# Next tiles' norms on ScalarE, sums stored through SP's queue, lower parts on VectorE, in the first pair of a one-core attention and FFN kernel

## The chip, the cores and the metric

The kernel runs on one core of a Trainium2 chip. The time is the device time in microseconds (us) of that core, and the median of several runs is given. A run with the hardware profiler stands beside them; its page counts the span from the first to the last instruction.

The engines are called PE (TensorE), ACT (ScalarE), DVE (VectorE), POOL (GpSimd) and SP (SyncE, which here only issues DMAs). Each works through its own instructions in order. An instruction that waits holds up all that stand behind it on its engine, and that includes the DMAs which the engine issues.

## What is computed

The input has 4096 tokens of 256 values. Linear attention comes first, then a feed-forward network, each followed by a residual and a layer norm:

```python
Q, K, V = x @ wq.T, x @ wk.T, x @ wv.T          # 64 wide
energy  = K.T @ V                               # over all tokens
x = layernorm(x + (Q @ energy) * sqrt(3 / 64) @ wo.T)
h = silu((x @ w1.T) * s1) * ((x @ w2.T) * s2)   # 1024 wide
h = gelu((h @ h1.T) * hs1)                      # 1024 x 1024
h = gelu((h @ h2.T) * hs2)                      # 1024 x 1024
x = layernorm(x + (h @ w3.T) * s3)
```

## The kernel before

**Tiles and pairs.** The tokens are cut into eight tiles of 512, and these into four pairs. The attention runs first for all tiles, up to `m2 = energy @ wo`; the queries are kept in `stk`, with an upper part in rows 0 to 63 and a lower part in rows 64 to 127. Each pair then goes through the gate (`w1`, `w2`, 32 products), two square layers and the last product with `w3`. While a pair is in its gate, the attention's output of the next pair's tiles is added to `x` (`attend_norm`'s `add`); while it is in its square layers, these tiles are normalised, transposed by DVE in blocks of 32 and moved into `xT` by many small DMAs (`moves`).

**Two parts.** Matmuls run in a reduced float32 form, so an operand is split in two: `hi`, a cast on ACT, and `lo`, the rest, on DVE (`convert`, L231 and L232). Each product runs once with either.

**Square layers.** A 1024 x 1024 layer for a pair (1024 columns) is a 2 x 2 block product with seven block products instead of eight (`square_layer`). `ORDER` gives the order of the weights: A11, A12, S2, S1, S3, A22, S4, where the S are sums of blocks. A product (L278) uses two blocks of weights of 0.5 MB, 16 pairs of a weight load and a matmul of 128 x 512 for each, and writes four PSUM banks. Products 1, 3, 5 and 6 share the banks `al` (6, 7, 4, 5), and ACT reads these out after each: copies at L347, L361 and L371, and after product 6 the GELU of L318. Products 2, 4 and 7 use `be` (0 to 3). The next layer's product 1 starts `al` anew.

**Weights.** `fetch` keeps five buffers `ws` filled. In pair 0 the blocks A11, A12 and A22 come from the inputs through POOL's queue (L267); all else comes from the scratch `sw` in DRAM through SP's queue (L269). The sums in `sw` are made in pair 0: `sums(layer, k)` has four DVE additions (L290) of raw blocks into two buffers `so` and two stores (L440, on POOL's queue). There are two buffers `so` in all, so that sum k+1 waits for the stores of sum k. Layer 0's sums are made in the attention and the gate of pair 0, layer 1's inside layer 0 (`second_sums`), with `raw_blocks` loading what k+2 needs.

**Background.** `fill(us)` takes jobs from a list and emits them at four places of a square layer, up to a budget that `FILL`, or `FIRST` in the first layer of pair 0, sets. A job is half a sum, half a norm or half a tile's transposes. All order is that of the program; nothing is rearranged.

**Norms.** `attend_norm` gives the steps: `stats` (L145, L147), `root` (L85 on DVE, then a power on POOL, L86) and `norm` (L167). In the jobs, `norm` runs on POOL, one pass of subtract and multiply per 128 tokens. The last pair's closing phase has another form (`norm_on_act`, L958 and L959): two passes on ACT, one with a negated mean as its bias and one with the root as its scale.

## Time and profile before

| | |
|---|---|
| median of 3 runs | 651.78 us (651.54 to 656.1) |
| profiled execution | 653.67 us, its span 651.9 us |
| PE busy | 631.8 us (97%) |
| DVE busy | 496.1 us (76%) |
| ACT busy | 381.4 us (59%) |
| POOL busy | 233.1 us (36%) |
| mean granted clock of PE | 0.987 |
| DMA moved | 113.44 MB, mean 174 GB/s |

Busy shares are means over the whole span; the stage that the change touches, the first square layer of pair 0, takes 51 us of it (72.7 to 123.4). In a line of a timeline the columns are: start, duration, engine, line, operation, the tiles written and read, shapes, count, and in brackets the idle time before it with what ended it. In a line of the waits: who waited for whom, the sum in us, how often, the longest. In a line of the groups: busy time and mean ns of one, then the idle time before the group. In the windows each engine has its busy time and count, and PEclk is the share of full clock that PE was granted.

### The profile page before, as it was taken

How to read it: one execution, taken by the hardware profiler on the slowest of the kernel's cores; microseconds unless marked ns; L12 is line 12 of the kernel's file. 1: busy time of each engine (PE TensorE's matmuls, PEld its weight loads, DVE VectorE, ACT ScalarE, POOL GpSimd, SP SyncE). 2: the span in 40 equal slices, each digit the busy share in tenths (PEclk: the TensorE clock that was granted, in tenths of full speed). 3: DMA queues.
4: the chain of work that ended last, by engine and by line, in shares of the span. 5: the costliest groups of instructions: out<-in, count | busy, mean ns of one | idle time of the engine just before them, and what ended most of it. 6: DMA issues, size and time to landing. Idle time of an engine off the chain costs nothing.

```text
span 651.9 us, 8976 instructions
## 1 busy us (share of the span) xinstructions
PE 631.8 (97%) x3163; PEld 533.6 (82%) x3163; DVE 496.1 (76%) x750; ACT 381.4 (59%) x522; POOL 233.1 (36%) x290
## 2 busy tenths in 40 slices
PE   8999999959999999999999999999999999999994
PEld 7878888848898888888898888888899888888894
DVE  3789986895475888698677988798767987588466
ACT  5546472645664455655684556766684556766564
POOL 1234117722814713632535722631645720000005
PEclk9999999979999999999999999999999999999998
DMA  8988749845853037764762125654860125644201
GB/s 335 330 300 246 244 144 364 268 155 182 250 152 103 33 137 247 268 218 167 225 191 71 60 97 171 216 183 154 248 190 4 65 98 173 215 150 141 98 1 67
DMA packets 58800, 113.44 MB, mean 174 GB/s; under 512 B 19488, under 2 KB 34528, under 8 KB 58368
## 3 DMA queue, kind: packets, MB, share of 16 engines
q1 hardware_dynamic: 40864, 73.56, 34.0%
q0 software_dynamic: 17520, 38.55, 18.6%
q10 hardware_dynamic: 368, 0.72, 0.3%
q8 instruction: 26, 0.43, 0.3%
q14 instruction: 22, 0.18, 0.1%
HBM read 97.08 MB, written 18.87 MB: 178 GB/s over the span
## 4 chain that ended last, share of the span: by engine, by line
PE 86%; DMA 5%; DVE 5%; POOL 1%; issue 1%; ACT 1%; SPq 0%; POOLq 0%; DVEq 0%; ACTq 0%
PE bank L278 53%; PE bank L611 18%; PE bank L755 9%; DMA sw<-so 3%; PE bank L507 2%; DVE f L290 2%; PE bank L528 1%; DMA ws<-in_h 1%; POOL x L167 1%; DVE so L290 1%; DMA f<-in_xt 1%; PE bank L518 1%; PE bank L137 1%; PE bank L138 1%; DVE lo L232 1%
## 5 line engine op out<-in xcount | busy, mean ns | idle before, releaser
L278 PE MATMUL bank<-hi,ws 128*128 128x512 f32 x896 | 350.3, 391 | 7.7 <-DMA ws<-in_h 7.7
L278 PE MATMUL bank<-lo,ws 128*128 128x512 f32 x896 | 349.9, 391 | 0.0
L232 DVE TENSOR_TENSOR lo<-f,hi 128x1024 fp32r<-128x1024 f32 x144 | 170.3, 1221 | 69.6 <-ACT hi L231 69.1
L278 PEld LDWEIGHTS bank<-hi,ws 128*128 128x128 f32 x896 | 169.0, 189 | 43.3 <-DVE f L290 8.1
L278 PEld LDWEIGHTS bank<-lo,ws 128*128 128x128 f32 x896 | 169.1, 189 | 35.2
L231 ACT CAST hi<-f 128x1024 fp32r<-128x1024 f32 x144 | 144.5, 1051 | 52.0 <-PE bank L278 26.9
L318 ACT ACTIVATE f<-f,hs 128x512 f32<-128x512 f32 x96 | 62.8, 715 | 71.7 <-DVE f L290 71.7
L611 PE MATMUL bank<-hi,w 128*128 128x512 f32 (+1 forms) x268 | 101.7, 383 | 1.0 <-DVE d L766 0.6
L611 PE MATMUL bank<-lo,w 128*128 128x512 f32 (+1 forms) x268 | 101.2, 381 | 0.1
L620 ACT ACTIVATE f<-bank,s 128x512 f32<-128x512 f32 x64 | 44.0, 690 | 65.6 <-PE bank L611 62.3
L290 DVE TENSOR_TENSOR f<-f,f 128x1024 f32<-128x1024 f32 x64 | 76.5, 1221 | 4.5 <-ACT f L318 3.8
L290 DVE TENSOR_TENSOR f<-f,bank 128x512 f32<-128x512 f32 x96 | 62.1, 681 | 21.8 <-ACT f L371 16.0
L767 POOL TENSOR_TENSOR x<-x,d 128x256 f32<-128x256 f32 x31 | 27.0, 897 | 114.0 <-DVE d L766 113.9
L621 DVE SCALAR_TENSOR_TENSOR f<-bank,s,f 128x512 f32<-128x512 f32 x64 | 47.7, 748 | 26.2 <-PE bank L611 23.6
L755 PE MATMUL bank<-w,lo 128*128 128x256 f32 x256 | 61.6, 283 | 0.0
L755 PE MATMUL bank<-w,hi 128*128 128x256 f32 x256 | 61.6, 283 | 0.0
L611 PEld LDWEIGHTS bank<-hi,w 128*128 128x128 f32 x268 | 50.4, 188 | 11.3 <-DVE d L766 1.0
L611 PEld LDWEIGHTS bank<-lo,w 128*128 128x128 f32 x268 | 50.4, 188 | 9.6 <-DVE lo L191 0.3
L216 POOL DMA_DIRECT2D xT<-x x96 | 52.2, 551 | 8.1 <-DMA stage<-in_h 3.0
L755 PEld LDWEIGHTS bank<-w,lo 128*128 128x128 f32 x256 | 49.1, 192 | 0.2
L755 PEld LDWEIGHTS bank<-w,hi 128*128 128x128 f32 x256 | 49.1, 192 | 0.2
L717 POOL DMA_DIRECT2D stage<-in_h x16 | 9.0, 561 | 107.8 <-DVE stage L743 104.0
(121 smaller groups left out, 553.1 us busy)
## 6 DMA issues: line engine op xcount, KB each, us to landing
ws<-sw SPq DMA_DIRECT2D x100, 512.0 KB, 3.3
sw<-so POOLq DMA_DIRECT2D x16, 512.0 KB, 5.4
stage<-in_h POOLq DMA_DIRECT2D x16, 512.0 KB, 5.0
ws<-in_h POOLq DMA_DIRECT2D x12, 512.0 KB, 7.4
sw<-in_h SPq DMA_DIRECT2D x12, 512.0 KB, 5.5
x<-in_x SPq DMA_DIRECT2D x16, 256.0 KB, 3.7
f<-in_xt SPq DMA_DIRECT2D x6, 512.0 KB, 7.8
f<-in_h SPq DMA_DIRECT2D x6, 512.0 KB, 10.3
```

Source lines behind the costliest of these rows:

```text
L216: moves.popleft()()
L231: nc.scalar.copy(hi[:, c, :], src[:, c, :])
L232: nc.vector.tensor_tensor(lo[:, c, :], src[:, c, :], hi[:, c, :].bitcast(F32), ALU.subtract)
L278: nc.tensor.matmul(ps[2 * h + o], w[:, k, o * P : (o + 1) * P], part[i][:, k, :], start=start and k == 0 and i == 0, stop=k == HK - 1 and ...
L290: engine.tensor_tensor(dst, u, v, op)
L318: nc.scalar.activation(dst, src, AF.Gelu, scale=sc[:, o : o + 1])
L507: nc.tensor.matmul(pk[:, s, :], x[:, k, s * P : (s + 1) * P], wkv[:, k, :], start=(k == 0), stop=(k == KE - 1),)
L611: nc.tensor.matmul(ps[:, c], w[:, k, o * P : (o + 1) * P], part[:, 2 * j + k, c], start=(k == 0 and i == 0), stop=(k == KE - 1 and i == 1),)
L620: nc.scalar.activation(g, pa, AF.Silu, scale=s1[:, o : o + 1])
L621: nc.vector.scalar_tensor_tensor(g, pb, s2[:, o : o + 1], g, ALU.mult, ALU.mult)
L755: nc.tensor.matmul(ps[:, :E], part[q][:, k, s * P : (s + 1) * P], w3[:, k0 + k, :], start=i % 2 == 0 and k == 0 and q == 0, stop=i % 2 == ...
L767: engine.tensor_tensor(y[:, s, :], y[:, s, :], d, ALU.add)
```

## The change

1. In the first pair the norms of tiles 2 and 3 leave POOL: `norm_on_act` does them on ACT in two passes, after both halves' statistics; DVE makes the negated mean (`minus_mean`).
2. `sums` stores through SP's queue. The two sums made in the attention stay on POOL's. `raw_blocks` for layer 1 goes through SP for k = 0 and 2 and through POOL for 1 and 3.
3. The lower parts of query tiles 3, 4 and 5 (`stack_lo`) move from POOL to DVE, and from ahead of the gate to inside its first products.
4. The jobs' order is k0, k1, norm 2, k2, transposes 2, k3, norm 3, transposes 3, where the transposes stood at the end; `FIRST` has other budgets.
5. The activation that loads the Silu table at a pair's end is issued after the tail's GELU and not ahead of it.

```diff
+        def norm_on_act(minus):
+            for s in range(NS):
+                nc.scalar.activation(
+                    y[:, s, :], x[:, s, :], AF.Identity, bias=minus[:, s : s + 1], scale=1.0
+                )
+                nc.scalar.activation(
+                    y[:, s, :], y[:, s, :], AF.Identity, scale=r[s // 2][:, s % 2 : s % 2 + 1]
+                )
+
+        def minus_mean():
+            m = p2.tile([P, NS], F32, tag="mm", name=f"mm{t}")
+            nc.vector.tensor_scalar(m, mv[:, :, 0], -1.0, None, ALU.mult)
+            return m
+
+        norm.on_act = norm_on_act, minus_mean
...
-    FIRST = {2: 2.8, 3: 5.4, 4: 2.8, 5: 5.4}
+    FIRST = {2: 2.8, 3: 5.8, 4: 4.4, 5: 5.8}
...
-    def sums(layer, k, raw):
+    def sums(layer, k, raw, queue=nc.sync):
...
-            nc.gpsimd.dma_start(
+            queue.dma_start(
                 out=sw[layer][2 * i : 2 * i + 2, :, :, k, :].rearrange("m h p o -> p m h o"),
...
     def stack_lo(t):
-        nc.gpsimd.tensor_tensor(
+        nc.vector.tensor_tensor(
             stk[t][D:P], qf[t][D:P], stk[t][D:P].bitcast(F32), ALU.subtract
         )
...
-                early = sums(0, t // 2 - 2, raws[t // 2 - 2])
+                early = sums(0, t // 2 - 2, raws[t // 2 - 2], nc.gpsimd)
...
-    for t in range(3, LATE):
-        stack_lo(t)
...
         if o == 1:
             turn(2, 4)
             split(2, 4)
+            for t in range(3, LATE):
+                stack_lo(t)
...
-            raw_blocks(1, 0, xTr, nc.gpsimd)
+            raw_blocks(1, 0, xTr)
...
-                raw_blocks(1, k + 2, later_raws[k % 2], nc.gpsimd)
+                raw_blocks(1, k + 2, later_raws[k % 2], (nc.sync, nc.gpsimd)[k % 2])
...
-    def attend_jobs(t):
+    def attend_jobs(t, on_act=False):
...
             root(g)
+            if on_act:
+                if g:
+                    norms, minus = norm.on_act
+                    norms(minus())
+                return
             for s in (2 * g, 2 * g + 1):
                 norm(s, nc.gpsimd)
...
-            (a0, a1), (a2, a3) = attend_jobs(ta + 2)
-            (b0, b1), (b2, b3) = attend_jobs(tb + 2)
+            (a0, a1), (a2, a3) = attend_jobs(ta + 2, p == 0)
+            (b0, b1), (b2, b3) = attend_jobs(tb + 2, p == 0)
...
-                background.extend((*k0, *k1, a0, a1, *k2, *k3, b0, b1, a2, a3, b2, b3))
+                background.extend((*k0, *k1, a0, a1, *k2, a2, a3, *k3, b0, b1, b2, b3))
...
-        if p + 1 < NP:
-            nc.scalar.activation(once, mhalf[:, :1], AF.Silu)
...
         tail()
+        if p + 1 < NP:
+            nc.scalar.activation(once, mhalf[:, :1], AF.Silu)
```

As the program is emitted, PE's order stays as it was. On ACT the eight passes of tile 2 stand between the casts of product 6's operand and those of product 7's, ahead of the copies L371; the eight of tile 3 stand after the casts of the next layer's first operand and ahead of the GELU that reads product 6's banks. On DVE the negated mean follows each tile's statistics, tile 2's transposes stand between the halves of sums 2 and 3, and tile 3's after its statistics.

## The prediction

> **What bounds the kernel now.** The page gives TensorE (PE) 97% of the span, and the chain that ended last is 86% PE. So only PE's holes can move the time, and I read the waits of PE first:

> ```profile
> PE bank L278 <- DMA ws<-in_h: 7.7, 1, 7.7
> ...
> PE bank L182 <- DVE x L167: 0.7, 1, 0.7
> ```

> There is one large hole, 7.7 us, in a matrix product of the square layers (L278) that waits for a weight block. The windows around it say when, and that it costs more than its length:

> ```profile
> core 0: us, PE busy (x) PEld busy (x) DVE busy (x) ACT busy (x) POOL busy (x), PEclk, DMA share, GB/s
> ...
> 134.00:138.00 4.00, 0.48 (x3) 0.06 (x1) 3.43 (x3) 2.33 (x3) 1.04 (x2) 0.88 0.93 287
> 138.00:142.00 4.00, 0.00 (x0) 0.00 (x0) 3.97 (x5) 3.99 (x7) 0.00 (x0) 0.50 0.30 77
> 142.00:144.00 2.00, 1.79 (x4) 1.49 (x5) 2.00 (x3) 0.00 (x0) 0.00 (x0) 0.50 0.03 8
> ```

> PEclk falls to 0.50 in the hole and stays there after it. In the chain, the 176 matmuls after the hole take 42.54 us, and at 101.55 us for 448 (the rate of the later pairs) they would take 39.9: the half clock costs 2.6 us more. The hole is worth **10.3 us**.

> The POOL timeline shows why the block came late:

> ```profile
> 125.85 3.83 POOL L167 TENSOR_SCALAR x<-x,mv,ra 128x256 f32<-128x256 f32 x2
> 129.65 0.71 POOL L86 TENSOR_TENSOR ra<-ra,mhalf 128x2 f32<-128x2 f32 x1
> 130.47 3.78 POOL L167 TENSOR_SCALAR x<-x,mv,ra 128x256 f32<-128x256 f32 x2
> 134.19 0.85 POOL L267 DMA_DIRECT2D ws<-in_h  x1
> ```

> The block's fetch (L267) is queued on POOL behind the norms of tile 3. It was issued at 134.2 and landed 7.9 us later; its buffer had been free since about 120.

> I count **half products** (16 matmuls, 3.63 us, one weight block each) from the first square layer of pair 0. Half 0 starts at 72.7, half 10 at 108.9, half 14 (the second layer) at 123.4. The hole stands before half 17. Half 10 begins product 6, half 14 the next layer's product 1. Both write the `al` banks, and both must first see ScalarE (ACT) read `al` out.

> **The change, part by part.**

> *POOL loses the norms of tiles 2 and 3 and the later sum stores.* The late block now stands behind seven small moves (L216, 0.55 each) and two powers (L86, 0.8 each), which wait for tile 3's statistics and are over by about 130; 8 us of landing gives 138. The hole before half 17 goes: **-10.3 us**.

> *Three lower parts (L550) move from POOL to DVE.* While POOL ran them (37.5 to 41.3), DVE's norm of tile 0 was slow and PE waited for it. In DVE's timeline:

> ```profile
> 34.80 0.74 DVE L167 TENSOR_SCALAR x<-x,mv,ra 128x256 f32<-128x256 f32 x2 [0.26 <-POOL ra L86]
> ...
> 37.44 2.75 DVE L167 TENSOR_SCALAR x<-x,mv,ra 128x256 f32<-128x256 f32 x2
> ```

> and in PE's timeline

> ```profile
> 40.25 0.55 PE L182 MATMUL bank<-ident,x 128*128 128x128 f32 x3 [0.74 <-DVE x L167]
> ```

> The same two norms took 0.74 and then 2.75. With POOL idle the second pair ends near 38.2, before the transposes at 39.24 need it. The 0.74 and the 0.18 after it go, and I leave 0.1 for the split that follows: **-0.8 us**. On DVE the three operations (0.69 each by L539, the same 64x512) stand before the first gate's product at 43.55, in an idle stretch of 1.2 us. The gates' three pairs of banks hide the rest. Without that cover it would be 0.9.

> *Stores through SP.* Two queues are concerned. SP's loads of `x` for tiles 2 and 3 now wait behind the sums of the gate phase: issued at about 62 instead of 40 and 52. Before, the transfers of those microseconds filled the DMA engines, the last of the two issued at 61.5 and 62.05 landing at 67.7. One 0.5 MB transfer replaces another there, so the first `x` lands at about 67.7, just as DVE wants it (67.8). PE needs the add done at 69.9, and it ended at 69.1: 0, at most 2. Later SP's weight loads (L269) wait behind stores: the second one of product 7 behind the third step's first store, at 112 for a use at 120. Hidden.

> Does a store land sooner from SP? [...] The rows show nothing: `sw<-so` from POOL 5.4 us median, `sw<-in_h` from SP 5.5, same size. [...]

> *Norms on ACT.* The price is in the closing phase, which has this very pair of passes:

> ```profile
> L959 ACT ACTIVATE x<-x,ro 128x256 f32<-128x256 f32 x7 | 3.6, 509 | 0.6 <-POOL ro L86 0.2
> L958 ACT ACTIVATE x<-x,minus 128x256 f32<-128x256 f32 x7 | 3.5, 499 | 5.8 <-DVE minus L967 5.8
> ```

> Eight passes are 4.0 us. Busy time isn't the matter, place is. In ACT's new order tile 2's passes stand before the casts of product 7's operand (L231, 2.0) and the copies out of `al` (L371). Tile 3's stand before the GELUs out of `al` (L318). Where these were, in ACT's timeline:

> ```profile
> 103.69 0.59 ACT L371 COPY f<-bank 128x512 f32<-128x512 f32 x1 [0.95 <-PE bank L278]
> ...
> 119.12 2.40 ACT L318 ACTIVATE f<-bank,hs 128x512 f32<-128x512 f32 x4
> ```

> and the work that makes the norms ready, in DVE's timeline:

> ```profile
> 102.80 0.69 DVE L290 TENSOR_TENSOR so<-stk 128x512 fp32r<-128x512 f32 x1 [0.60 <-DMA sw<-so]
> ...
> 106.08 0.24 DVE L85 TENSOR_SCALAR ra<-mv 128x2 f32<-128x2 f32 x1
> ```

> ACT was idle there, but the norms are not ready there: the statistics stand on DVE behind sums 0 and 1, which wait for their buffers to be stored.

> Hole A, before half 10. Statistics end at 106.3 (the DVE row, and a negated mean of 0.15). Passes 4.0: 110.3. Casts 2.0: 112.3. First copy 0.59: 112.9. PE wanted it at 108.9, so it waits 4.0.

> Hole B, before half 14. DVE goes on when the casts are there: that operand's lower part to 114.2 (L232, ending 1.9 after the first cast); second half of sum 2 to 115.5 (two L290, 1.3); four transposes, moved up, to 117.0 (L815, 8.7/24 each); first half of sum 3 to 118.4; four adds of C22 to 120.9. Before, from the start of these adds to the end of the lower part of the next operand was 6.6 (114.05 to 120.66): 125.0. Second half of sum 3 to 126.3; statistics of tile 3 as at 123.70 to 126.08, and 0.15, to 128.8. Passes 4.0: 132.8. First GELU 0.68: **133.5**, where half 14 began at 123.4. So the second layer starts 10.1 later. Hole A, and a half clock after it, lie inside this, since the chain goes through DVE and ACT.

> PE is empty from about 129 to 133.5. What does the clock do? [...] The trace fell to half 2.6 us after the last matmul's end (134.5 to 137.0, from the 0.88) and lost 2.6. I take the row, 2.5. [...]

> *Silu load after the tail, FIRST, turn of queues.* Each of three pairs loses two table loads (1.28 each) on ACT; no wait of PE at a pair's turn names ACT, so 0. FIRST and the job order are already in the order used above.

> **Sum.** -10.3 - 0.8 + 10.1 + 2.5 = +1.5; the second layer's third product needs its operand at about 149, which the slow halves hide. Half 14's bounds: 130.6 if the stores land at once, so that statistics end at 104.0 (DVE's own work) and both chains shorten; 138 if two of the waited stores take 8.4 us, the slowest landing of this row, and not 4.7 to 5.7. That is -1.4 to +6, and up to 2 more for the `x` loads. Between, I allow 0.3 for an earlier issue (POOL issued the first store at 95.9, DVE had it ready at 95.6): **+1.2**. The profiled execution, 653.67 us (span 651.9), would be 654.9; the runs' median, 651.78, becomes **653.0**.

> **Rivals.**
> 1. *ScalarE hides the norms* (7%). Then both holes are absent: 651.8 - 11.1 = 640.7. For it: ACT is busy 59%, and sat idle 5.0 us before 114.76. Against: DVE's own work lets no passes start before 104, and 4 + 2 + 0.6 after that is 110.6, past 108.9.
> 2. *The stores are the bound* (16%). Sums 0 and 1, and then 2 and 3, share buffers; each step waits for a landing. From 98 to 112 the DMA engines are full (share 1.06 in that window from 100), and raw blocks, weights and stores now come from two queues. If two landings slip to 8.4 us and the `x` loads cost 1.5, half 14 starts at 138.5 and the sum is +8.0: 659.8. It decides, and makes the kernel slower by over 1%, from half 14 at 138.5, or at 137 with that delay of `x`.
> 3. *Forecast* (77%): hole 17 traded for holes A and B, 649 to 658.

> **How the numbers follow.** One per cent, 6.5 us, is about what a measurement of this kernel can tell from no change. Faster 0.07 is rival 1; slower 0.16 is rival 2, with the later `x` loads; same 0.77. The range, 648.5 to 660.5, takes in the bounds of half 14 (650.4 to 657.8), the `x` loads and rival 2's 659.8.

> **What would show it.** Waits of PE: no `ws<-in_h`, instead ACT before products 6 and 1, about 4 and 4.5 us; PEclk 0.50 near 130 to 137; ACT rows of L318 out of `bank` after eight passes, near 133; the transpose at 40.25 without its wait. I am wrong if PE has no hole at half 14, if its hole comes from a DMA, or if PE waits for `x` at 68.

## The result, and the profile after

The changed kernel takes 660.98 us (659.01 to 663.14) beside 651.66 of the kernel before: a ratio of 1.0139, with a 95% interval of 1.0097 to 1.0182. It is **slower by 1.4%**. The forecast was 653.0 with a range that ended at 660.5. The profiled execution took 662.13 us, its span 660.35, 8.5 more than before.

The waits of PE, who waited for whom, us in total, times, longest:

```profile
PE bank L294 <- ACT f L334: 6.6, 1, 6.6
...
PE bank L294 <- ACT f L387: 3.3, 1, 3.3
```

The wait of 7.7 us for `ws<-in_h` is gone, and so is the one of 0.7 before the transpose. In their place stand holes A (for the copies out of `al`, L387, which was L371) and B (for the GELUs out of `al`, L334, which was L318). The windows around hole B:

```profile
core 0: us, PE busy (x) PEld busy (x) DVE busy (x) ACT busy (x) POOL busy (x), PEclk, DMA share, GB/s
...
132.00:136.00 4.00, 0.00 (x0) 0.00 (x0) 1.75 (x8) 2.79 (x7) 3.57 (x6) 0.90 1.06 276
136.00:140.00 4.00, 2.39 (x6) 1.91 (x7) 0.89 (x2) 3.97 (x8) 3.71 (x8) 0.50 0.63 140
```

PE stands empty to 137.6, and the clock is at half there. ACT's timeline shows the eight passes ahead of what PE waits for, twice:

```profile
107.98 0.51 ACT L175 ACTIVATE x<-x,mm 128x256 f32<-128x256 f32 x1 [8.83 <-DVE mm L184]
...
111.88 1.97 ACT L247 CAST hi<-f 128x1024 fp32r<-128x1024 f32 x2
113.76 2.04 ACT L387 COPY f<-bank 128x512 f32<-128x512 f32 x4
...
133.00 0.51 ACT L175 ACTIVATE x<-x,mm 128x256 f32<-128x256 f32 x1 [5.05 <-DVE mm L184]
...
136.89 2.41 ACT L334 ACTIVATE f<-bank,hs 128x512 f32<-128x512 f32 x4
```

From the first pass to the next work is 3.9 us each time (4.0 were worked out). But the second block starts at 133.0, and DVE's timeline says why so late:

```profile
107.78 0.16 DVE L184 TENSOR_SCALAR mm<-mv 128x4 f32<-128x4 f32 x1
115.33 0.69 DVE L306 TENSOR_TENSOR so<-xT 128x512 fp32r<-128x512 f32 x1 [7.39 <-DMA sw<-so]
116.06 0.69 DVE L306 TENSOR_TENSOR so<-so,xT 128x512 fp32r<-128x512 f32 x1
116.67 2.35 DVE L248 TENSOR_TENSOR lo<-f,hi 128x1024 fp32r<-128x1024 f32 x2
...
132.80 0.16 DVE L184 TENSOR_SCALAR mm<-mv 128x4 f32<-128x4 f32 x1
```

DVE is idle for 7.4 us until a sum's buffer has been stored. The lower part of product 7's operand (L248) stands behind that sum, although its casts were over at 113.85. The transfers issued in that stretch, after first (KB each, median us to landing), and the same two stores in before:

```profile
sw<-so SPq DMA_DIRECT2D x2, 512.0 KB, 11.3
stk<-in_h POOLq DMA_DIRECT2D x2, 512.0 KB, 8.5
ws<-sw SPq DMA_DIRECT2D x1, 512.0 KB, 8.3
```

```profile
sw<-so POOLq DMA_DIRECT2D x2, 512.0 KB, 8.2
```

Last, the end of the chain of waits under its heading, which gives the span, after and then before:

```profile
core 0 of [0], span 660.4 us
...
652.95 0.06 DVE flag L1026
```

```profile
core 0 of [0], span 651.9 us
...
647.83 0.06 DVE flag L1006
```

The last work ends 5.1 us later, the program 8.5 us later. At the end POOL runs an instruction of the program's closing block, a drain, which begins 1.1 us before the last work is over in both kernels and which the rest of the closing block follows. Its row in the trace has 7.62 us, where it was 4.27; no view lists it by name.

Where the 8.5 us are (half products counted as in the prediction):

| stretch | before | after | difference | predicted |
|---|---|---|---|---|
| start to half 0 | 72.66 | 74.58 | +1.9 | -0.8 |
| half 0 to half 14 | 50.78 | 63.03 | +12.3 | +10.1, less 0.3 allowed |
| half 14 to the last matmul of pair 0's square layers | 60.93 | 52.74 | -8.2 | -10.3 + 2.5 |
| from there to the last matmuls | 462.93 | 462.07 | -0.9 | 0 |
| last matmuls to the end | 4.58 | 7.93 | +3.4 | 0 |

Each kernel was profiled once more (`b_again` and `a_again`, below). Between those two executions the same rows are -0.8, +12.6, -5.7, -0.5 and +3.4, together +9.0. So the second and the last row repeat to 0.4 us; the first and the third do not.

### The profile page after: what moved, and what is told of

Same layout as the page of the kernel before. It is cut to its first block, busy times and chain, and to the rows that moved or that the text cites. A ratio compares the mean times of both kernels' runs of the same rounds, so it can differ in the third digit from the quotient of the medians.

```text
span 660.4 us, 8984 instructions
## 1 busy us (share of the span) xinstructions
PE 636.1 (96%) x3163; PEld 537.5 (81%) x3163; DVE 496.6 (75%) x755; ACT 380.1 (58%) x532; POOL 204.3 (31%) x263
## 4 chain that ended last, share of the span: by engine, by line
PE 84%; DVE 6%; DMA 4%; ACT 2%; issue 2%; SPq 0%; POOLq 0%; POOL 0%; DVEq 0%; ACTq 0%
PE bank L294 54%; PE bank L625 15%; PE bank L771 9%; PE bank L523 3%; DMA sw<-so 2%; DVE f L306 1%; DVE lo L248 1%; PE bank L544 1%; DVE so L306 1%; DMA x<-in_x 1%; DMA f<-in_xt 1%; DVE f L635 1%; ACT f L334 1%; PE bank L534 1%; ACT hi L247 0%
## 5 line engine op out<-in xcount | busy, mean ns | idle before, releaser
L248 DVE TENSOR_TENSOR lo<-f,hi 128x1024 fp32r<-128x1024 f32 x144 | 170.0, 1221 | 68.3 <-ACT hi L247 67.6
L334 ACT ACTIVATE f<-f,hs 128x512 f32<-128x512 f32 x96 | 62.7, 715 | 73.6 <-DVE f L306 73.6
L783 POOL TENSOR_TENSOR x<-x,d 128x256 f32<-128x256 f32 x31 | 27.9, 928 | 131.8 <-DVE d L782 131.7
L232 POOL DMA_DIRECT2D xT<-x x96 | 52.4, 553 | 6.9 <-DMA stage<-in_h 3.5
```

The source lines that it names most:

```text
L232: moves.popleft()()
L248: nc.vector.tensor_tensor(lo[:, c, :], src[:, c, :], hi[:, c, :].bitcast(F32), ALU.subtract)
L334: nc.scalar.activation(dst, src, AF.Gelu, scale=sc[:, o : o + 1])
L783: engine.tensor_tensor(y[:, s, :], y[:, s, :], d, ALU.add)
```

## The experiments

Profiled executions are read by the row; times are medians. "+63.0" is a start counted from half 0.

**Both kernels again.** `b_again` is the kernel before, `a_again` the changed one, unedited.

> The kernel before, unchanged, profiled a second time. The changed kernel's profile differed from that of before at two ends that the change does not touch: PE's clock came up at 12.3 us and not at 3.9 (first products 3.2 us later), and POOL's closing drain took 7.6 us and not 4.3. Theory: both are luck of the execution, so here either may differ from the first profile by about 3 us, with the 7.7 us hole before half product 17 unchanged. Rival: both belong to the kernels, and here the clock comes up at 3.9 and the drain takes 4.3 again.

> The changed kernel, unchanged, profiled a second time. Theory (luck at both ends): holes before half products 10 and 14 again near 3.3 and 6.6 us, while the clock's first rise and the closing drain may be anywhere (drain 4 to 8 us). Rival (they belong to the kernel): rise near 12.3 us and drain near 7.6 us again. The time should stay 1.2 to 1.6 per cent over before in either case.

`b_again` 652.48 us (ratio 1.0007, 0.999 to 1.0023), `a_again` 660.06 (1.0109, 1.0076 to 1.0141). The drain is 4.27 again in the one and 7.62 in the other, so it belongs to the kernels, as the rival had it. Half 14 of `a_again` starts at +63.4. What does vary within one kernel is the first rise of the clock (at 3.9 and 10.3 us in the two executions of before, 12.3 and 9.0 in the two of after), and with it the start of the gate (36.79 and 38.48; 40.02 and 37.95; from 36.1 to 40.0 in all sixteen executions of this document). The hole before half 17 varies too: in `b_again`

```profile
PE bank L278 <- DMA ws<-in_h: 5.6, 1, 5.6
```

since its fetch landed in 5.6 us and not in 7.9. Pair 0's square layers ended at 183.9 there and at 184.4 in the first execution, which had begun its gate 1.7 sooner. So the first row's +1.9 holds 3.2 us of chance, in the start of the gate, and a gain of 1.3 from there to half 0. In `a_again` that gain is only 0.2: there the four loads of `x` behind SP's stores landed at 69.5 to 71.4, and PE waited 0.7 us for an add of `x`. The prediction had that cost at 0, at most 2.

**Norms on ScalarE alone.** `e_act`: the kernel before with `norm_on_act` and `minus_mean` for the first pair, nothing else.

```diff
-            (a0, a1), (a2, a3) = attend_jobs(ta + 2)
-            (b0, b1), (b2, b3) = attend_jobs(tb + 2)
+            (a0, a1), (a2, a3) = attend_jobs(ta + 2, p == 0)
+            (b0, b1), (b2, b3) = attend_jobs(tb + 2, p == 0)
```

> The kernel before with one part of the change: the first pair's norms of tiles 2 and 3 on ScalarE in two passes; stores, job order, budgets and lower parts as before. Theory: the passes' place on ScalarE makes both new holes: PE waits for ScalarE about 4 us before half product 10 and 4 to 6 us before half product 14, the hole at 17 is gone; time +1 to +3 us (653 to 655). Rival (the stores through SP make the holes): no hole over 1 us at 10 and 14, time 641 to 643.

654.08 us, ratio 1.0031 (1.0015 to 1.0048). Its waits:

```profile
PE bank L294 <- ACT f L387: 3.6, 1, 3.6
PE bank L294 <- ACT f L334: 3.1, 1, 3.1
```

Hole 17 is gone and A and B are there, so both are ACT's and the trade of one hole for two is this edit's. Half 14 is at +59.6, 3.5 earlier than in the changed kernel's first execution. After hole B the clock stayed full: 1.00 in both windows there, where the second of the two at A has 0.70. The windows around A and around B:

```profile
108.00:112.00 4.00, 0.86 (x4) 0.38 (x2) 0.98 (x1) 3.88 (x8) 0.79 (x1) 1.00 1.05 412
112.00:116.00 4.00, 3.54 (x11) 2.78 (x12) 3.96 (x7) 1.87 (x4) 0.77 (x1) 0.70 1.02 315
128.00:132.00 4.00, 0.88 (x5) 0.38 (x4) 0.00 (x0) 3.84 (x9) 0.84 (x2) 1.00 0.85 250
132.00:136.00 4.00, 4.00 (x18) 3.29 (x19) 1.36 (x2) 3.56 (x5) 0.00 (x0) 1.00 0.15 59
```

**Stores and raw blocks on SP alone.** `e_sp`:

```diff
-            nc.gpsimd.dma_start(          # in sums.store
+            queue.dma_start(              # nc.sync; the two early sums keep nc.gpsimd
...
-            raw_blocks(1, 0, xTr, nc.gpsimd)
+            raw_blocks(1, 0, xTr)
...
-                raw_blocks(1, k + 2, later_raws[k % 2], nc.gpsimd)
+                raw_blocks(1, k + 2, later_raws[k % 2], (nc.sync, nc.gpsimd)[k % 2])
```

> The kernel before with one part of the change: the sums' stores and half of the raw blocks through SP's queue; norms stay on GpSimd. Theory: the stores wait behind raw blocks and a weight load in SP's queue while the second queue takes half of the engines, so that the third step's first addition starts 3 to 5 us later (110.4 before), tile 3's norms follow, and the hole at 17 grows from 7.7 to 10 to 12 us: 654 to 656. Rival (all issuers share the engines, a store lands as before): hole 7 to 8, time 651 to 652.5.

656.96 us, ratio 1.0073 (1.005 to 1.0097). The two stores of sum 1 took

```profile
sw<-so SPq DMA_DIRECT2D x2, 512.0 KB, 10.7
```

so the late landing comes with this edit. From 104 to 107, where they were issued, the two queues' packets had 59.2 and 49.8% of the 16 engines; in before one queue alone had 101.9% from 101.5 to 105, where the same two took 8.2. But the hole before half 17 is 5.4 us, no longer than in `b_again`, and the last matmuls start at 647.5, as in before (647.3). The time went into the drain, 7.62 us. I had not expected that of this part.

**The changed kernel with the stores and raw blocks back on POOL.** `e_after_pool`:

```diff
-    def sums(layer, k, raw, queue=nc.sync):
+    def sums(layer, k, raw, queue=nc.gpsimd):
...
-            raw_blocks(1, 0, xTr)
+            raw_blocks(1, 0, xTr, nc.gpsimd)
...
-                raw_blocks(1, k + 2, later_raws[k % 2], (nc.sync, nc.gpsimd)[k % 2])
+                raw_blocks(1, k + 2, later_raws[k % 2], nc.gpsimd)
```

> The changed kernel, with the later sums' stores and all raw blocks of the second layer put back on POOL's queue; norms on ScalarE, lower parts on VectorE stay. Theory 'SP's queue costs twice' (sum stores land at 10.8 us behind xT's raw block and weight loads, and POOL's closing drain is 7.6 instead of 4.3): the first store of sum 1 lands in 8 to 9 us, the third sum starts about 2 us sooner, the hole before half 14 falls from 6.5 to about 4, the drain is 4.27, and the time is 660.9 - 3.35 - 2.5 = 655, between 653 and 656. Rival 'the queue doesn't matter, the chain through VectorE alone is longer than I worked out': landing and drain stay, hole B stays at 6 to 6.5, time 659 to 661.

656.19 us (654.14 to 658.73), ratio 1.0073 (1.0046 to 1.01), so by the medians 4 to 5 us of the change are this part. Its own division was only half right. The stores of sum 1 still took 9.3 and 9.9 us, hole B is 5.9 and half 14 at +61.8, a gain of 1.3 to 1.6 and not 2.5. The drain is 3.29, but POOL must then wait for SP, which stands still from 653.5 to 655.9 (a fetch of instructions, at 654.4, falls in that time), so that from the last matmuls to the end there are 6.6 us. This execution was the slowest of the nine; no trace shows whether the others end so.

**Norms on VectorE in the changed kernel.** `e_after_dve`:

```diff
-            if on_act:
-                if g:
-                    norms, minus = norm.on_act
-                    norms(minus())
-                return
...
-                norm(s, nc.gpsimd)
+                norm(s, nc.vector if on_act else nc.gpsimd)
```

> The changed kernel, with the norms of tiles 2 and 3 on VectorE (tensor_scalar, as in before on POOL) instead of two passes on ScalarE; stores on SP, job order and FIRST stay as changed. Theory 'the two ScalarE blocks make both holes': no hole over 1.5 us before half products 10 and 14 and no half clock after 14, so 660.9 - 3.3 - 6.5 - 2.3 = about 649; the drain is 7.6 and the store landing 10 to 11 as before, and neither makes a hole. Rival 'the late store makes hole B by itself' (through the statistics and lower parts on VectorE): the hole before half 14 stays at 4 or more and the time is 655 or more.

656.97 us, ratio 1.0085 (1.0056 to 1.0115): the rival's time, with its hole before half 12 and not before 14. Only 1.5 us are ACT's now (L363, in the second layer), but

```profile
PE bank L294 <- DVE f L306: 5.5, 1, 5.5
```

and in DVE's timeline

```profile
113.36 0.69 DVE L306 TENSOR_TENSOR so<-xT 128x512 fp32r<-128x512 f32 x1 [4.62 <-DMA sw<-so]
114.09 0.69 DVE L306 TENSOR_TENSOR so<-so,xT 128x512 fp32r<-128x512 f32 x1
114.69 2.35 DVE L248 TENSOR_TENSOR lo<-f,hi 128x1024 fp32r<-128x1024 f32 x2
...
120.80 2.47 DVE L306 TENSOR_TENSOR f<-f,bank 128x512 f32<-128x512 f32 x4
```

The sum waits for the store, the operand waits for the sum, transposes and more sums follow, and the adds of C22, for which product 7 waits, come at 120.8. So the wait for the store makes a hole of its own when ACT's are gone.

**Is it the landing or the order of the jobs?** `f_jobs`: the changed kernel with the old order and budgets.

```diff
-    FIRST = {2: 2.8, 3: 5.8, 4: 4.4, 5: 5.8}
+    FIRST = {2: 2.8, 3: 5.4, 4: 2.8, 5: 5.4}
...
-                background.extend((*k0, *k1, a0, a1, *k2, a2, a3, *k3, b0, b1, b2, b3))
+                background.extend((*k0, *k1, a0, a1, *k2, *k3, b0, b1, a2, a3, b2, b3))
```

> The changed kernel with the jobs' order and FIRST as before (transposes of tile 2 after both sums; 5.4, 2.8, 5.4); norms on ScalarE, stores on SP, lower parts on VectorE stay. In the changed kernel the first half of the third sum, which waits for the late store, stands ahead of the lower part of product 7's operand, and transposes and half of the fourth sum stand ahead of C22's adds. Theory 'the late store costs what it does because of that order': with the old order the lower part no longer waits for the store, half 14 begins 59.5 to 60.5 us after half 0 (63.0 to 63.4 in the changed kernel, 59.6 in e_act), the time is 657 to 658, and the closing drain stays 7.6. Rival 'the late store alone': half 14 at 62 to 63, time 660 to 661.

658.2 us, ratio 1.0091 (1.0073 to 1.011), half 14 at +60.2, both as the theory had it. The stores land as late as in the changed kernel (11.0 and 11.8 us), but now the operand is ahead:

```profile
110.69 2.36 DVE L248 TENSOR_TENSOR lo<-f,hi 128x1024 fp32r<-128x1024 f32 x2 [5.00 <-ACT hi L247]
113.28 0.69 DVE L306 TENSOR_TENSOR so<-xT 128x512 fp32r<-128x512 f32 x1 [0.23 <-DMA sw<-so]
```

DVE waits 0.2 us for the store where it waited 7.4, and hole B is 3.0. In the program it is `FIRST[3]` of 5.8 that lets one more job, the waiting half sum, in ahead of the operand; this budget was not run alone. The order and the queue add up like this: half 14 at +63.0 and +63.4 with both new, +61.8 with the new order and stores from POOL (`e_after_pool`), +60.2 with the old order and stores from SP (`f_jobs`), +59.6 with neither (`e_act`, whose lower parts are still on POOL, ahead of half 0). So the order is the larger part, and the late store costs most where the order lets something wait for it.

**Lower parts alone.** `e_lo`: the kernel before with `stack_lo` on `nc.vector`, its three calls inside the first gate products.

> The kernel before, with only the three lower parts moved from POOL to VectorE (inside the first gate products). Theory as in the prediction: the wait of 0.7 us before the transpose at 40.25 goes and half 0 begins 0.8 sooner. If the fetch behind POOL's norms is set by what VectorE and POOL do after half 0, the gain stays, 651; if it is set by the statistics, which follow stores counted from the gate phase, the hole before half 17 moves with it and the gain stays too; if the hole is set by absolute time it swallows the gain: 651.7. All theories 650.5 to 652; over 653 would say that VectorE's three operations cost in the gate phase what the prediction put at nothing.

649.88 us, ratio 0.9975 (0.9958 to 0.9992). From the first gate matmul to half 0 it takes 34.32 us, and 34.56 in the changed kernel's first execution, where before took 35.87. The part is good for 1.3 to 1.5 us in the trace, not 0.8, and hole 17 doesn't swallow it. The three operations, here in `e_best` below, are

```profile
42.39 1.90 DVE L550 TENSOR_TENSOR stk<-qf,stk 64x512 fp32r<-64x512 f32 x3
```

and PE has no wait there.

**Norms and lower parts on VectorE, all else as before.** `e_dve` is `e_lo` with

```diff
-                norm(s, nc.gpsimd)
+                norm(s, engine)              # nc.vector in the first pair
```

and `e_best` has the last slot of the first layer shortened as well:

```diff
-    FIRST = {2: 2.8, 3: 5.4, 4: 2.8, 5: 5.4}
+    FIRST = {2: 2.8, 3: 5.4, 4: 2.8, 5: 2.8}
```

> The kernel before, with the three lower parts on VectorE within the first gate products and the first pair's norms on VectorE instead of POOL; job order, FIRST, stores on POOL and the Silu load as before. Theory (hole 17 is POOL's norms ahead of a weight fetch; the holes A and B are ScalarE's passes; the drain belongs to the stores on SP): the hole before half 17 goes, no hole over 1.5 us takes its place, drain 4.27, span 651.1 - 8 to 11 = 640 to 643, time 641 to 645. Rival 'VectorE's chain is the next bound': 8 norms of 0.37 us (3 us, or 11 if they run at 1.4 each as beside POOL) stand before the lower parts of products' operands, a hole of 3 us or more opens before half 10 or 14, time 646 or more.

> e_dve with one number changed: the first layer's last slot of jobs, FIRST[5], is 2.8 instead of 5.4, so that the statistics and norms of tile 3's first halves (5.5 us of VectorE at 121.8 to 127.3 in e_dve, 1.8 of it waiting for POOL's powers) move into the second layer's slots. Theory: they stand ahead of the lower part at 127.3 and make e_dve's hole of 1.7 at 130.3, and the backlog the one of 1.8 at 139.7; both go, and the time is 647.5 - 2 to 3.5 = 644 to 645.5. Rival: the work only comes later and holds the lower parts of the second layer's operands up there; holes of the same sum, 647 to 649.

`e_dve` 647.53 us, ratio 0.9944 (0.9929 to 0.996): half 10 and half 14 are on time (+36.3 and +50.8) and hole 17 is gone, but the statistics and norms of tile 3 hold the second layer up in two holes of 1.7 and 1.8. The rival was right about the time and about what is in the way, though it looked for the hole before half 10 or 14; these are before halves 16 and 18. `e_best` **641.93 us, ratio 0.9852 (0.9812 to 0.9892)**, clearly faster than both kernels, more than I had expected of that one number. Its longest waits of PE:

```profile
PE bank L1005 <- DVE ok L864: 3.8, 1, 3.8
PE bank L492 <- DVE warm L396: 1.3, 1, 1.3
PE bank L507 <- DMA f<-in_xt: 0.9, 1, 0.9
PE bank L755 <- DVE lo L232: 0.6, 2, 0.4
```

None of the waits lies in pair 0's square layers, and the clock is full from 9.2 us to the closing phase (mean 0.996). On DVE two norms are one row:

```profile
106.94 0.73 DVE L167 TENSOR_SCALAR x<-x,mv,ra 128x256 f32<-128x256 f32 x2 [1.85 <-POOL ra L86]
```

0.73 us for what took POOL 3.83 and ACT 2.0, and no second pass.

**The closing drain.** Three variants of the kernel before: `d_moves` puts the 16 small moves of the last tile from POOL on SP, `d_store` the later sums' stores, `d_raw` the raw blocks (the two edits of `e_sp`, one at a time).

```diff
-                            (nc.sync, nc.gpsimd)[len(moves) % 2].dma_start,
+                            (nc.sync, nc.gpsimd)[t != NT - 1 and len(moves) % 2].dma_start,
```

> The kernel before, with the 16 small moves of the last tile that POOL issues put on SP: 149 transfers issued by POOL in all instead of 165, as in the changed kernel, with stores and raw blocks on POOL as before. If POOL's closing drain follows the number of transfers that POOL issues, it is 7.6 us instead of 4.27 and the span is 3.3 us longer than before's 651 to 652. If it belongs to the stores or to which transfers they are, it stays 4.27. A third value would say that it depends on more than the number.

> The kernel before, with the later sums' stores on SP, and the raw blocks left on POOL: 153 transfers issued by POOL. If the stores land late because the raw block xT and the weights stand ahead of them in SP's own queue, they land in about 8 us here (9 before, 10.8 with both on SP); if they land late because they share the engines with whatever POOL's queue holds, 10 or more here too. Drain: 7.6 if it belongs to the stores, between 4.27 and 7.6 if it grows as the count falls.

> The kernel before, with the raw blocks of the second layer put on SP as in the changed kernel, and the stores left on POOL: 161 transfers issued by POOL. If the order within one queue decides, the stores land as before in 8 to 9 us, since only small things stand ahead of them on POOL; the drain 4.27 if it belongs to the stores, slightly more than 4.27 if it grows as the count falls.

| kernel | transfers issued by POOL | later sums' stores on | drain, us |
|---|---|---|---|
| before, `b_again`, `e_act`, `e_lo`, `e_dve`, `e_best` | 165 | POOL | 4.27 |
| `e_after_pool` | 165 | POOL | 3.29 |
| `d_raw` | 161 | POOL | 3.38 |
| `d_moves` | 149 | POOL | 2.97 |
| `d_store` | 153 | SP | 7.95 |
| after, `a_again`, `e_sp`, `e_after_dve`, `f_jobs`, `f_best_sp` | 149 | SP | 7.62 |

The number of transfers doesn't decide it; the stores do, in seven executions of seven. How stores that have landed by 135 us come to lengthen POOL's drain at the program's end, no view shows, and I leave it open. The three were run once each: 655.27, 656.96 and 655.83 us. These times don't follow the drain alone: `d_moves` has a wait of PE of 3.8 us for `d` at 498.7, and `d_raw` has waits of 1.8 and 2.1 us at 70.9 and 131.7, which before has not. On the landing the three say less. With the stores alone or the raw blocks alone on SP, the stores of sum 1 are issued later (up to 110 us) and take 5.6 to 6.9. The last of them has landed at +40.9 in both, beside +40.2 and +40.7 in the two executions of before, and +42.1 with both edits (`e_sp`). So, in one execution each, neither edit alone made it late.

**The drain in a kernel without holes.** `f_best_sp`: `e_best` with `e_sp`'s edit.

> e_best with the later sums' stores and half of the second layer's raw blocks on SP, as in the changed kernel. Theory 'stores on SP cost the closing drain wherever they stand, and the late landing costs PE nothing where no operand waits behind it': drain 7.6, no hole over 1.5 us in pair 0, time 641.9 + 3.4 = 645.3, between 644.5 and 646.5. Rival 'the late store makes a hole by itself': a hole of 2 us or more before half 12 to 17, time 648 or more. If the drain were 4.3 here, it would not belong to the stores on SP.

647.49 us, ratio 0.9938 (0.9919 to 0.9956), slower than expected by one. The drain is 7.62, and PE has one hole, of 0.8, before half 12 (half 14 at +52.0, 1.2 later than in `e_best`), with the stores taking 9.6 and 11.1 us. From the drain 3.35 and from the landing 1.2 make 4.6 of the 5.6 us between the two medians.

## Why the prediction was wrong

**What held.** Hole 17 went; the stretch after half 14 lost 8.2 us where 7.8 was worked out. Holes A and B came where ACT's order put them. In A every step held: taking off the later start of half 0 (1.9), the statistics were over at 106.0 (106.3), the passes at 110.1 (110.3), the casts at 111.9 (112.3), the first copy at 112.4 (112.9); A is 3.3 us (4.0). The clock after B cost 2.2: the 224 matmuls from half 14 on take 50.54 in `e_best` and 52.74 here. The prediction had 2.5, from the trace of before.

**The mis-sized term: the wait for the store in hole B.** The step reads "that operand's lower part to 114.2 (L232, ending 1.9 after the first cast); second half of sum 2 to 115.5". It took the first half of that sum as done, as in before, where it ran at 110.4. In the changed order this half stands ahead of the lower part, and it started at 113.4 on the same scale, because its store took 10.8 us. The lower part ended at 117.1, 2.9 late, and what follows kept nearly all of it: second half sum 118.3 (115.5), transposes 119.6 (117.0), C22's adds 123.3 (120.9), statistics 131.0 (128.8), passes 135.1 (132.8), half 14 at 135.7 (133.5), 2.2 late. The prediction had a store at "5.4 us median" from POOL and "5.5" from SP and concluded that "the rows show nothing". Medians over a whole program hid the two stores that something waits for: they took 7.9 to 9.1 us from POOL in the two executions of before and 10.8 to 12.5 from SP in the two of after. Of the 2.2 us, `e_after_pool` gives 1.3 to the queue; the other 0.9 stay with the stores on POOL, where they took 9.3 and 9.9. Without the new order the late stores cost little: half 14 is at +60.2 in `f_jobs`, beside +59.6 in `e_act`. Rival 2 named the mechanism and priced it with 8.4 us, the slowest landing of the row from POOL; the point that it gave for deciding, 138.5, wasn't reached on its scale.

**The missed term: the end.** The prediction costed the stores' change of queue by what waits behind them. It had no line for the drain at the program's end, a term left at nothing without a reason, and measured it is 3.35 us in each execution. It is the largest part of the miss that repeats. That the stores' queue decides the drain is shown; how it does so is open, and nothing in before's trace pointed to it.

**Smaller ones.** The lower parts gave 1.3 where 0.8 was set, save in `a_again`, where the `x` loads took most of it back. The wait of 0.6 us for `d` (L766) at 202.5 in before didn't recur, part of the -0.9. And the hole before half 17 was 7.7 us long in the execution that the sum was made against, 5.4 to 5.6 in `b_again`, `e_lo` and `e_sp`: priced by one execution, which had also begun its gate early, the gain of 10.3 is some 2 us too large for one like `b_again`'s. The third row is -8.2 against the execution that the sum was made from, and -5.7 between the second executions.

Together, from the forecast of +1.2, for the first pair of profiles: the landing 2.2, the 0.3 allowed for an earlier issue, which came with no earlier landing, the drain 3.4, the start 3.2, less 0.5 for the lower parts, 0.9 later on and 0.4 of the third row: +8.5.

## What to carry to other kernels

A median landing time can hide the transfer that a buffer waits for (before's stores had a median of 5.4 us, the two of sum 1 a median of 8.2): read the landing of that one, in its own stretch, and ask what stands in both queues then. Work that may wait for a transfer belongs behind the operands of the next product on its engine, not ahead; one job more in a budget made 0.2 us of waiting into 7.4. Before passes are moved off a busy engine, price each engine that has gaps at the right place: the norms of the two tiles took 13.7 us on POOL, 8.0 on ACT and 3.0 on DVE, and on DVE they were not in the way once tile 3's were put off by one slot.

## What the runs showed of the hardware

| trace | step, us | PE busy, us | clock in the step | clock after it |
|---|---|---|---|---|
| before | 133.6 to 137.0 | 0.85 | full | half |
| before | 137.0 to 140.5 | 0.00 | half | half |
| before | 140.5 to 143.9 | 1.65 | half | half |
| before | 143.9 to 147.3 | 3.41 | half | full |
| before, closing phase | 642.2 to 645.6 | 1.25 | full | half |
| after | 111.3 to 114.7 | 0.30 | full | half |
| after | 114.7 to 118.1 | 3.41 | half | full |
| after | 131.8 to 135.2 | 0.00 | full | half |
| after | 135.2 to 138.6 | 0.98 | half | half |
| after | 138.6 to 142.0 | 3.41 | half | full |
| after, closing phase | 647.2 to 650.6 | 1.41 | full | half |

All other steps at full clock had 2.33 us or more, and no fall came after them. So the step ahead of a fall was empty in one case of five. The two holes of like length in `e_act`, 3.6 and 3.1 us, cost differently: the clock fell after A, and stayed full after B. How PE's work lay in the steps around them is not shown here.

**One DVE row beside POOL.** The second two norms of tile 0 took DVE 2.75 to 2.77 us in before, `b_again` and `e_act`, where POOL ran the lower parts at the time, and 0.73 to 0.74 in `e_lo`, `e_dve`, `e_best`, after and `a_again`, where it didn't. PE waited 0.7 to 0.8 us for the norms in the first three, and also in `e_sp` and the three drain variants, which keep the lower parts on POOL.

**POOL's closing drain** took 3.0 to 4.3 us where POOL issued the later sums' stores (nine executions) and 7.6 to 8.0 where SP did (seven), and was the same in both executions of each kernel that was profiled twice.
